# At most two indirect transfers under way, and a plan that reckons with it

## The chip, the cores and the metric

The kernel runs on one core of one Trainium2 chip, as one launch. The metric is the device time in microseconds, from three runs of the kernel. A core has TensorE (PE in the profile), VectorE (DVE), ScalarE (ACT) and GpSimd (POOL), each with its own queue of instructions that it executes in order, SyncE (SP), which here only issues transfers, and 16 DMA engines that all queues share.

## What is computed

A tensor of 32 images with 128 channels and 56 x 56 points goes through two layers. Cut to what matters:

```python
x = x + conv3x3(sign(group_norm(x)), sign(w)) * Alpha
t = to_tokens(x)                                  # 3136 tokens of 128 per image
n = layer_norm(t)
kv = sum over tokens of (n @ Wk + bk) * (n @ Wv + bv)
t = t + (n @ Wq + bq) * kv
n = layer_norm(t)
p = softmax(n @ router_w + router_b)              # 8 experts
top 2 of p, made to sum to 1
t = t + sum over the two: p_e * (n @ expert_w[e] + expert_b[e])
out = from_tokens(t)
```

## The kernel before

An image's 3136 tokens stand in 25 chunks of 128 (the last one has 64). Experts are computed in two ways. **Dense**: for the first 12 chunks of the images 0 to 27, and for all 25 chunks of the last four images, every expert is applied to every token, with the gate (0 for most) multiplied in first: the gates are spread over the partitions by a transfer (`bc`, line 1000), VectorE multiplies (`gated`, line 1009), TensorE multiplies with the expert's weights (`ff`, line 1027). **Sorted**: the other 13 chunks of the images 0 to 27 are sorted by their pair of experts. Each row is written to a place of its own in a table in HBM by an indirect transfer, one for each chunk (`scatter`, line 1202: `rows<-tok,row_no`); the images form four groups of 8, 8, 8 and 4; once a group is complete its tiles of 128 rows are loaded, transposed, multiplied with the two experts of their pair (lines 1440 to 1509) and written to a second table `res`; and a second indirect transfer for each chunk (`gather`, line 1272: `back<-res,res_no`) brings each token's row back, which is transposed (`back_ps`, line 1286), copied (`o`, line 1294) and stored.

So there are 28 x 13 = 364 scatters and as many gathers. All are issued by POOL[...]. POOL's other work is the inverse root of the variance of the two layer norms, a power with the exponent -1/2: `rstd1` and `rstd2` of each image, 64 instructions `r<-var,m_half` of line 449. `rstd1` is needed by `scaled` (ACT, line 624) and by `project_out` (ACT, line 762), `rstd2` by the routing (`route_1`, DVE, line 836) and what follows from it: gates, places of rows, scatters.

The order of work is made in two stages. The kernel records **steps** with `at(due, key, engine, work, ...)`: `work` is the time that the plan reckons on the engine, `delay` what passes after it until others may use the result, `after` what must be done before, and `take`/`free` the buffers it takes and gives back. `in_order` (line 108) goes through the steps as the engines would and brings them into one list: of the steps that can start within 0.3 us of the earliest, the one with the smallest due time comes first. The program is then recorded in that order, and the framework places the instructions on each engine's queue. It takes the recorded order as a preference and not as a rule, so that the built program's order on an engine is not quite that of the plan. The framework also puts in the semaphore waits. The transfers of POOL's queue use eight semaphores in turn, and in the built program a transfer waits for the one eight before it.

Buffers that bear on the change: a gather takes one of six `back` buffers, given back by `back_turn` on PE; the scatters read the token tile `tok`, of which there are three.

Of the kernel before, what the change touches and what calls it, by code (L numbers as in the profile page):

```python
# [67 lines left out]
N_PAIR = N_EXP * (N_EXP - 1) // 2  # L68
N_DENSE = 12
GROUPS = (8, 8, 8, 4)  # L70
TILE_PACE = (0.7, 0.6, 0.4, 0.3)
GATHER_PACE = (1.0, 0.8, 0.5, 0.4)
N_Q = C + 2 * N_EXP
# [82 lines left out]
def conv_attn_moe_kernel(  # L156
# [19 lines left out]
    nc = tc.nc  # L176
# [203 lines left out]
    before = const.tile([C, C], BF16, name="before")  # L380
# [47 lines left out]
    def at(due, key, engine, work, do, *args, after=(), take=(), free=(), delay=0.0):  # L428
        steps[key] = Step(due, key, engine, work, do, args, after, take, free, delay)
# [24 lines left out]
    def plan_image(i: int):  # L454
        s = base(i)
        d = {}
# [41 lines left out]
        def gn_sign(r0, r1):  # L498
# [9 lines left out]
            after=[("load", i - 1)] + ([("gn_sign", 0, GN_PARTS - 1)] if i == 1 else []),  # L508
            take=["x"], delay=9.0 if i else 19.0,
        )  # L510
        for j in range(GN_PARTS):
            rows = j * height // GN_PARTS, (j + 1) * height // GN_PARTS
# [3 lines left out]
                after=[("gn_neg", i), ("conv", i - 1, min(j + 1, n_conv - 1))],  # L516
# [3 lines left out]
            after=[("gn_sum", i, j) for j in range(GN_PARTS)],  # L520
# [4 lines left out]
            after=[("gn_mean", i), ("gn_sign", i - 2, GN_PARTS - 1)], free=[("tr", ("gn_mean", i))],  # L525
# [56 lines left out]
        for b in range(n_conv):  # L582
            at(
                s + 5.5 * b, ("conv", i, b), "PE", 1.75, conv, b,
                after=[("gn_sign", i, j) for j in range(min(b + 2, GN_PARTS))]
# [5 lines left out]
                after=[("conv", i, b)], free=[("mm", ("conv", i, b))],  # L591
            )
        for g in range(n_blk):
            b = min(n_conv - 1, (cols_of(g)[1] - 1) // (ROWS * width))
            due = s + 4 + 5.5 * b
# [3 lines left out]
                after=[("conv_add", i, b), ("xt", i, g - 1)],  # L599
# [4 lines left out]
                after=[("xt", i, g)], free=[("tr", ("xt", i, g))],  # L604
# [3 lines left out]
                after=[("xt_out", i, g), ("var1", i - 2)],  # L608
# [3 lines left out]
            after=[("stats1", i, g) for g in range(n_blk)]  # L612
            + [("project_out", i - 2, 8), ("rstd1", i - 2)],
        )
        at(s + 44, ("rstd1", i), "POOL", 4.5, rstd1, after=[("var1", i)])


        def scaled(g):
# [83 lines left out]
        for g in range(n_blk):  # L702
# [3 lines left out]
                after=[("rstd1", i), ("scaled", i, g - 1), ("scaled", i - 1, last_b)], take=["y"],  # L706
# [3 lines left out]
                after=[("scaled", i, g), ("gram", i, g - 1), ("kv_7", i - 1)],  # L710
# [4 lines left out]
            after=[("gram", i, last_b), ("kv_8", i - 1)], free=[("acc", ("gram", i, 0))],  # L715
# [5 lines left out]
        for j, (engine, work, do) in enumerate(kv_steps, 1):  # L721
            after = [(f"kv_{j - 1}", i) if j > 1 else ("gram_out", i)]
# [9 lines left out]
        for g in range(n_blk):  # L732
# [3 lines left out]
                after=[("kv_4", i), ("scaled", i, g), ("stats1", i, g)],  # L736
# [46 lines left out]
        for j, cs in enumerate(q_groups):  # L783
# [4 lines left out]
                after=[("kv_8", i), ("project", i, j - 1)] + biased, take=["mm"],  # L788
# [4 lines left out]
                after=[("project", i, j)], take=["qs"], free=[("mm", ("project", i, j))],  # L793
# [131 lines left out]
        def gate_parts():  # L925
# [22 lines left out]
            after=[("project_add", i, j) for j in range(last_q + 1)]  # L948
            + [("dense_gates", i - 2), ("row_scalars", i - 2)],
        )  # L950
        at(s + 119, ("rstd2", i), "POOL", 4.5, rstd2, after=[("var2", i)])
        at(s + 125, ("route_1", i), "DVE", 0.85, route_1, after=[("rstd2", i)] + routed)
        at(s + 126, ("route_2", i), "DVE", 1.7, route_2, after=[("route_1", i)])
        at(s + 128, ("route_3", i), "DVE", 1.53, route_3, after=[("route_2", i)])
# [4 lines left out]
            after=[("route_5", i), ("gate_turn", i - 1)],  # L959
# [3 lines left out]
            after=[("dense_gates", i)], take=["tr"],  # L963
# [3 lines left out]
            after=[("gate_turn", i), ("gate_parts", i - 1), ("spread", i - 2, n_units - 1)],  # L967
            delay=3.0,
# [3 lines left out]
            after=[("gate_out", i)], free=[("tr", ("gate_turn", i))], delay=4.0,  # L972
# [72 lines left out]
        for b in dense_blocks:  # L1045
            share = (cols_of(b)[1] - cols_of(b)[0]) / WIDE
            n = b * pairs
            at(
                begin + n * unit - 4, ("tt_turn", i, b), "PE", 0.45 * share, to_channels, b,
                after=[("project_add", i, c // Q_GROUP) for c in blocks[b]]  # L1050
# [6 lines left out]
                after=[("tt_turn", i, b)], free=[("tr", ("tt_turn", i, b))],  # L1057
            )
            for k in range(pairs):
                n = b * pairs + k  # L1060
                at(
                    begin + n * unit - 12, ("spread", i, n), "SP", 0.1 + 0.3 * (k == 0), spread, b, k,
                    after=[("gate_out", i), ("spread", i, n - 1), ("spread", i - 1, last_unit)]
# [5 lines left out]
                    after=[("spread", i, n), ("tt_out", i, b)]  # L1069
# [6 lines left out]
                    after=[("gated", i, n), ("experts", i, n - 1)],  # L1076
# [5 lines left out]
                after=[("experts", i, n)],  # L1082
# [7 lines left out]
        group = group_of[i]  # L1090
# [106 lines left out]

        def scatter(c):
            n = rows_of(c)
            alone(  # L1200
                f"rows{group}",
                nc.gpsimd.indirect_dma_start(  # L1202
                    out=groups[group]["rows"],
                    out_offset=bass.IndirectOffsetOnAxis(
                        ap=d["row_no"][:n, c - N_DENSE : c - N_DENSE + 1], axis=0
                    ),
                    in_=d["tok"][:n, c, :],
                    in_offset=None,
                ),
            )  # L1210

        at(
            s + 132, ("pair_of", i), "DVE", 0.87, pair_of,
            after=[("route_3", i), ("row_numbers", i - 1), ("places", i - 1), ("result_rows", i - 14)],
# [3 lines left out]
            after=[("pair_of", i), ("count_rest", i - 1), ("list_1", group - 1)], take=["to"],  # L1218
# [5 lines left out]
            after=[("places", i), ("count_on", i), ("scatter", i - 2, n_ck - 1)],  # L1224
# [4 lines left out]
            after=[("route_5", i), ("row_add", i - 2, n_ck - 1)],  # L1229
        )  # L1230
        for k, c in enumerate(range(N_DENSE, n_ck)):
            at(
                s + 138 + 3 * k, ("row_add", i, c), "ACT", 0.30, row_add, c,
                after=[("row_scalars", i), ("row_numbers", i), ("project_add", i, c // Q_GROUP)],
                take=["sent"],
            )
            at(
                s + 140 + 3 * k, ("scatter", i, c), "POOL", 1.6, scatter, c,
                after=[("row_add", i, c), ("row_numbers", i), ("open", group)],
                free=[("tok", ("xt", i, 0)), ("sent", ("row_add", i, c))], delay=3.0,  # L1240
            )
        if first_of_group:
            at(
                s + 100, ("open", group), "SP", 0.2, open_group, group,
                after=[("prepare_sorted",), ("rstd1", i)]
# [23 lines left out]
        def gather(c):  # L1269
            d["back", c] = bpool.tile([C, C], F32, tag="back", bufs=6, name=f"back_{i}_{c}")  # L1270
            n = rows_of(c)
            nc.gpsimd.indirect_dma_start(  # L1272
                out=d["back", c][:n, :],
                out_offset=None,
                in_=groups[group]["res"][: quads_of(group) * WIDE, :],
                in_offset=bass.IndirectOffsetOnAxis(
                    ap=d["res_no"][:n, c - N_DENSE : c - N_DENSE + 1], axis=0
                ),
            )

        def back_turn(b):
            lo, hi = cols_of(b)
# [8 lines left out]
        def back_out(b):  # L1291
# [5 lines left out]
        begin, each = gather_due(group)  # L1297
        due = begin + each * (i - last_of[group] + GROUPS[group] - 1)
        at(
            due - 8, ("result_rows", i), "DVE", 1.55, result_rows,  # L1300
            after=[("list_2", group), ("gather", i - 2, n_ck - 1), ("result_rows", i - 1)],
        )
        k = 0
        for b in range(N_DENSE // PER, n_blk):
            share = len(blocks[b]) / PER
            for c in blocks[b]:
                at(
                    due + each * k / n_sort, ("gather", i, c), "POOL", 1.6, gather, c,
                    after=[("result_rows", i)]
                    + [("gather", i, c - 1) if k else ("gather", i - 1, n_ck - 1)]  # L1310
                    + [("tile_out", group, q) for q in range(quads_of(group))],
                    take=["back"], delay=3.0,
                )
                k += 1
            at(
                due + each * k / n_sort + 5, ("back_turn", i, b), "PE", 0.45 * share, back_turn, b,
                after=[("gather", i, c) for c in blocks[b]], take=["tr"],
                free=[("back", ("gather", i, c)) for c in blocks[b]],
            )
            at(  # L1320
                due + each * k / n_sort + 6, ("back_out", i, b), "ACT", 0.47 * share, back_out, b,
                after=[("back_turn", i, b)], free=[("tr", ("back_turn", i, b))],
            )


    groups = {}

    def alone(key, dma):

        tc.declare_no_dep(dma.ins, group=key, reason="writes rows of its own")  # L1330
        tc.add_to_no_dep_group(key, dma.ins)

    def tiles_of(g):
        return (GROUPS[g] * img_rows + N_PAIR * (C - 1)) // C

# [296 lines left out]
```

## Time and profile before

| | |
|---|---|
| time, median of 3 runs (lowest to highest) | 2934.11 us (2931.47 to 2934.41) |
| profiled execution: span, mean granted TensorE clock | 2897.8 us, 0.904 |
| PE busy | 2345.1 us, 81% |
| DVE busy | 1982.0 us, 68% |
| ACT busy | 1348.4 us, 47% |
| POOL busy | 1105.6 us, 38% |
| DMA, mean over the span | 161 GB/s |

A row of the profile's table of groups gives a line, an engine and an operation, how often it ran, its busy time and mean duration, and the idle time of the engine just before it with what ended that idle time. For a transfer that POOL issues the duration is that of the issuing instruction; when the data has landed is not part of it. The list of waits gives, for an engine and a line, what it waited for, the sum in us, how often, and the longest.

### The profile page before, as it was taken

The numbers are of one execution on the slowest core, as the hardware profiler recorded it, in microseconds if no ns is written. First come the engines' busy times: TensorE is split into PE (matmuls) and PEld (weight loads), VectorE is DVE, ScalarE is ACT, GpSimd is POOL, SyncE is SP. The second block draws the span as 40 slices with busy tenths as digits, with TensorE's granted clock in tenths as the row PEclk, the third lists the DMA queues.
The fourth block names the chain that finished last, engine by engine and source line by source line (L and its number), as shares of the span: only waits on it lengthen the run. The fifth ranks groups of instructions, "written<-read, shape, count | busy, mean of one in ns | idle before, by whom it ended". The sixth has DMA issues, their size and how long they took to land. (4 is left out here: it accounts for less than half of the span.)

```text
span 2897.8 us, 43587 instructions
## 1 busy us (share of the span) xinstructions
PE 2345.1 (81%) x11990; PEld 1537.8 (53%) x11990; DVE 1982.0 (68%) x5998; ACT 1348.4 (47%) x4211; POOL 1105.6 (38%) x908
## 2 busy tenths in 40 slices
PE   5888987788788788768887878878778768989777
PEld 3555554455555565536555655545556544655433
DVE  3887877687767678656667657667657657777564
ACT  5564544455544455434555455544446344443210
POOL 1352433321222224443433343665533244233454
PEclk9999999998898899889898989989989988989889
DMA  3354444455444454444554454545645455756476
GB/s 133 107 169 137 159 150 141 140 171 161 143 142 148 139 169 150 149 156 148 161 159 152 146 153 157 169 158 174 184 130 185 138 165 181 227 162 223 160 232 219
DMA packets 309729, 467.06 MB, mean 161 GB/s; under 512 B 61129, under 2 KB 209009, under 8 KB 309490
## 3 DMA queue, kind: packets, MB, share of 16 engines
q1 hardware_dynamic: 285186, 414.11, 45.0%
q0 software_dynamic: 23296, 46.64, 5.4%
q10 hardware_dynamic: 1008, 3.54, 0.4%
q8 instruction: 100, 1.64, 0.2%
q14 instruction: 139, 1.14, 0.1%
HBM read 345.73 MB, written 118.39 MB: 160 GB/s over the span
## 5 line engine op out<-in xcount | busy, mean ns | idle before, releaser
L1027 PE MATMUL ff<-gated,ew_d 128*128 128x512 f32 (+1 forms) x1792 | 895.5, 634 | 123.7 <-DVE gated L1009 123.0
L1272 POOL DMA_INDIRECT back<-res,res_no x364 | 412.6, 1133 | 688.4 <-PE back_ps L1286 551.0
L1202 POOL DMA_INDIRECT rows<-tok,row_no x364 | 395.9, 1088 | 561.5 <-ACT gt_parts L918 174.6
L1027 PEld LDWEIGHTS ff<-gated,ew_d 128*128 128x128 f32 x1792 | 345.4, 207 | 479.2 <-issue 296.2
L1009 DVE TENSOR_TENSOR gated<-tt,bc 128x1024 f32<-128x1024 f32 (+1 forms) x448 | 526.4, 1182 | 92.5 <-PE ff L1027 45.4
L449 POOL TENSOR_TENSOR r<-var,m_half 128x25 f32<-128x25 f32 x64 | 287.6, 4499 | 534.1 <-DVE var L445 516.0
L533 PE MATMUL cv<-xs,w_bin 128*128 128x448 bf16 x2016 | 454.1, 373 | 25.3 <-ACT xs L499 11.2
L624 ACT ACTIVATE y<-tok,r 128x128 f32<-128x128 f32 (+1 forms) x800 | 251.8, 394 | 202.3 <-POOL r L449 180.1
L762 ACT ACTIVATE qs<-q,r 128x136 f32<-128x136 f32 (+1 forms) x800 | 244.7, 388 | 197.2 <-PE q L748 170.3
L533 PEld LDWEIGHTS <-w_bin 128*128 128x128 bf16 x2016 | 206.1, 103 | 211.7 <-issue 73.2
L1465 PE MATMUL to<-ew_s,turned 128*128 x1856 | 263.7, 289 | 49.2 <-ACT turned L1453 32.2
L1465 PEld LDWEIGHTS to<-ew_s,turned 128*128 128x128 f32 x1856 | 243.7, 201 | 94.3 <-ACT turned L1453 43.1
L1480 ACT ACTIVATE v<-to,t_in 128x128 f32<-128x128 f32 x464 | 184.8, 456 | 230.0 <-PE to L1465 124.2
L748 PE MATMUL q<-move,x 128*128 128x144 f32 (+1 forms) x1600 | 251.5, 296 | 15.7 <-ACT move L691 5.1
L748 PEld LDWEIGHTS q<-move,x 128*128 128x128 f32 (+1 forms) x1600 | 222.0, 193 | 62.8 <-issue 32.1
L633 PE MATMUL gram<-y 128*128 128x129 f32 (+1 forms) x1600 | 219.9, 284 | 22.0 <-ACT y L624 22.0
L1492 DVE SCALAR_TENSOR_TENSOR v<-to,t_in,v 128x128 f32<-128x128 f32 x464 | 139.2, 342 | 141.3 <-ACT v L1480 102.9
L633 PEld LDWEIGHTS gram<-y 128*128 128x128 f32 (+1 forms) x1600 | 202.9, 195 | 60.7 <-ACT y L624 30.7
L544 DVE SCALAR_TENSOR_TENSOR x<-cv,alpha_col,x 128x448 f32<-128x448 f32 x224 | 150.8, 675 | 103.1 <-remote 43.9
L573 DVE BATCH_NORM_STATS2 st<-tok 128x6 f32<-128x128 f32 (+1 forms) x800 | 177.8, 276 | 52.1 <-ACT tok L566 30.2
L566 ACT COPY tok<-xt 128x512 f32<-128x512 f32 (+1 forms) x224 | 121.2, 558 | 156.9 <-PE xt L560 78.9
L781 DVE BATCH_NORM_STATS2 st<-tok 128x6 f32<-128x128 f32 (+1 forms) x800 | 180.3, 275 | 0.0
(208 smaller groups left out, 2787.8 us busy)
## 6 DMA issues: line engine op xcount, KB each, us to landing
bc<-gp SPq DMA_DIRECT2D x432, 512.0 KB
x<-in_x_dram SPq DMA_DIRECT2D x64, 784.0 KB
t_in<-rows SPq DMA_DIRECT2D x464, 66.0 KB
res<-v SPq DMA_DIRECT2D x116, 256.0 KB
out_dram<-tt SPq DMA_DIRECT2D x108, 256.0 KB
out_dram<-o SPq DMA_DIRECT2D x84, 256.0 KB
gt<-gb SPq DMA_DIRECT2D x324, 24.0 KB
rows<-zeros SPq DMA_DIRECT2D x116, 66.0 KB
```

What stands on the lines that cost most here:

```text
L449: nc.gpsimd.tensor_tensor(dst, var, m_half.to_broadcast([C, n_ck]), ALU.pow)
L533: nc.tensor.matmul(cv, lhsT=w_bin[:, t, :], rhs=xs[:, b * ROWS + dy : b * ROWS + dy + ROWS, dx : dx + width], start=(t == 0), stop=(t == T ...
L624: nc.scalar.mul(y[:n, j, :C], d["tok"][:n, c, :C], d["r1"][:n, c : c + 1])
L633: nc.tensor.matmul(d["gram"], lhsT=y[:n, j, :C], rhs=y[:n, j, :], start=(c == 0), stop=(c == n_ck - 1),)
L748: nc.tensor.matmul(p[:n, k, :], lhsT=d["x"][:, c * C : c * C + n], rhs=move, start=True, stop=True,)
L762: nc.scalar.mul(qs[:n, k, : C + N_EXP], p[:n, k, : C + N_EXP], d["r1"][:n, c : c + 1])
L1009: nc.vector.tensor_tensor(g[:, :, :n], d["tt", b][:, :n].unsqueeze(1).to_broadcast([C, 2, n]), d.pop(("bc", b, k))[:, :, :n], ALU.mult,)
L1027: nc.tensor.matmul(d["ff", b][:, :n], lhsT=ew_d[:, e * C : (e + 1) * C], rhs=g[:, j, :n], start=False, stop=(e == N_EXP - 1),)
L1202: nc.gpsimd.indirect_dma_start(out=groups[group]["rows"], out_offset=bass.IndirectOffsetOnAxis(ap=d["row_no"][:n, c - N_DENSE : c - N_DENS ...
L1272: nc.gpsimd.indirect_dma_start(out=d["back", c][:n, :], out_offset=None, in_=groups[group]["res"][: quads_of(group) * WIDE, :], in_offset= ...
L1465: nc.tensor.matmul(p[:, k, j, :], lhsT=t[:, n * C : (n + 1) * C], rhs=ew_s[:, bass.ds(d["cols", q][j][n], C)], start=True, stop=True,)
L1480: nc.scalar.activation(d["v", q][:, 2 * h + k, :], d["to", q, h][:, k, 0, :], AF.Identity, bias=row[:, C + 2 : C + 3], scale=row[:, C : C ...
```

## The change

The change has three parts.

1. `in_turn` adds to every indirect transfer a dependence on the one two before it (`IN_FLIGHT = 2`): it is issued only when that one has landed, so that at most two are under way. It holds for scatters and gathers together, in the order in which they are recorded.
2. The plan reckons 2.0 us of POOL's time for a scatter or a gather, where it was 1.6.
3. The plan lets 3.0 us (`rstd1`) and 6.0 us (`rstd2`) pass after the power before its result counts as ready; it was 0.

The second and third part change no instruction. They change the order in which steps are recorded. What it is for: that the transfers do not stand in each other's way, and that the plan places the work after the powers where the chip will have their results.

```diff
+IN_FLIGHT = 2
...
-        at(s + 44, ("rstd1", i), "POOL", 4.5, rstd1, after=[("var1", i)])
+        at(s + 44, ("rstd1", i), "POOL", 4.5, rstd1, after=[("var1", i)], delay=3.0)
...
-        at(s + 119, ("rstd2", i), "POOL", 4.5, rstd2, after=[("var2", i)])
+        at(s + 119, ("rstd2", i), "POOL", 4.5, rstd2, after=[("var2", i)], delay=6.0)
...
         def scatter(c):
...
+            dma = nc.gpsimd.indirect_dma_start(
...
+            alone(f"rows{group}", dma, in_turn(dma))
...
-                s + 140 + 3 * k, ("scatter", i, c), "POOL", 1.6, scatter, c,
+                s + 140 + 3 * k, ("scatter", i, c), "POOL", 2.0, scatter, c,
...
         def gather(c):
...
+            dma = nc.gpsimd.indirect_dma_start(
...
+            in_turn(dma)
...
-                    due + each * k / n_sort, ("gather", i, c), "POOL", 1.6, gather, c,
+                    due + each * k / n_sort, ("gather", i, c), "POOL", 2.0, gather, c,
...
+    def in_turn(dma):
+
+        before = moved[-IN_FLIGHT:][:1] if len(moved) >= IN_FLIGHT else []
+        for b in before:
+            tc.add_manual_dep(dma.ins, b.name, in_turn_dep, reason="few under way")
+        moved.append(dma.ins)
+        return before
```

More of the change, by code (lines that the diff above doesn't have):

```diff
@@ L1199, in scatter @@
             n = rows_of(c)
[L1200 to L1208, printed above, removed]
-                ),
+            dma = nc.gpsimd.indirect_dma_start(
+                out=groups[group]["rows"],
+                out_offset=bass.IndirectOffsetOnAxis(
+                    ap=d["row_no"][:n, c - N_DENSE : c - N_DENSE + 1], axis=0
+                ),
+                in_=d["tok"][:n, c, :],
+                in_offset=None,
             )
+            alone(f"rows{group}", dma, in_turn(dma))
         at(
@@ L1271, in gather @@
             n = rows_of(c)
-            nc.gpsimd.indirect_dma_start(
+            dma = nc.gpsimd.indirect_dma_start(
                 out=d["back", c][:n, :],
@@ L1326, in conv_attn_moe_kernel, with alone @@
     groups = {}
-    def alone(key, dma):
-        tc.declare_no_dep(dma.ins, group=key, reason="writes rows of its own")
+    def alone(key, dma, keep=()):
+        tc.declare_no_dep(dma.ins, group=key, keep=list(keep), reason="writes rows of its own")
         tc.add_to_no_dep_group(key, dma.ins)
+    in_turn_dep = mybir.DependencyInfo(mybir.DependencyClass.Sync, mybir.DependencyReason.DATA)
+    moved = []
+    def in_turn(dma):
[4 more added lines that the diff above has]
+        return before
     def tiles_of(g):
```

## The prediction

> **What bounds the kernel now.** I read the page's busy times first, then the groups of POOL's queue, then the list of waits. From the page (busy us, share of the span, instructions), and then its three groups of POOL:
>
> ```profile
> PE 2345.1 (81%) x11990; PEld 1537.8 (53%) x11990; DVE 1982.0 (68%) x5998; ACT 1348.4 (47%) x4211; POOL 1105.6 (38%) x908
> ...
> L1272 POOL DMA_INDIRECT back<-res,res_no x364 | 412.6, 1133 | 688.4 <-PE back_ps L1286 551.0
> L1202 POOL DMA_INDIRECT rows<-tok,row_no x364 | 395.9, 1088 | 561.5 <-ACT gt_parts L918 174.6
> L449 POOL TENSOR_TENSOR r<-var,m_half 128x25 f32<-128x25 f32 x64 | 287.6, 4499 | 534.1 <-DVE var L445 516.0
> ```
>
> PE is the busiest engine and idles 2898 - 2345 = 553 us; POOL works 38% of the span. POOL is not the bound: a change to its queue counts only through those who wait for POOL. They are in the list of waits (us in total, times, longest):
>
> ```profile
> ACT y L624 <- POOL r L449: 180.1, 32, 15.3
> DVE logit L836 <- POOL r L449: 165.8, 30, 10.6
> PE ff L1027 <- DVE gated L1009: 123.0, 37, 11.5
> PE back_ps L1286 <- DMA back<-res,res_no: 43.9, 20, 6.2
> PE gram L633 <- ACT y L624: 22.0, 14, 4.5
> ```
>
> ACT waits for `rstd1` 32 times, 5.6 us each, and DVE for `rstd2` 30 times, 5.5 us each: little more than one power of 4.5 us. So the powers seldom stand behind transfers; their own duration is waited for, once an image. PE feels this second hand: 123 us for `gated` (DVE stands in the routing), 22 us behind `scaled`. The gathers are waited for by PE only 44 us; mostly POOL waits for PE to give `back` buffers back (551 us).
>
> How long is a transfer under way? The trace's records of the software queue (23296 packets, 32 for each of the 728 transfers) show 16 of data and 16 of 4 bytes that close a transfer. From the start of POOL's instruction to the last closing packet a scatter takes 2.0 us (median; 90%: 3.4), a gather 3.2 us (90%: 5.7). At the start of an instruction 0, 1, 2, 3, 4, 5 earlier ones are still under way 97, 428, 147, 35, 20 and 1 times. So 203 of 728 would meet the new limit; the other 525 would not.
>
> **What the Trainium skill says.** "DMA: Bandwidth & Descriptors", section on the anatomy of one DMA on the SWDGE path, puts the fixed cost at about 2.0 us, mostly completion, and says that DMA engines do not wait on semaphores: a wait is made by the issuing sequencer. The 2.0 us of a scatter agrees; the gathers' 3.2 us is more. That a wait holds POOL itself no transfer here shows, as the wait for the one eight before never binds (five at most are under way); I take it as stated: what stands behind a held transfer on POOL is held too. "Perfetto Trace Analysis", section on SWDGE DMA instructions, says that the instruction ends with its descriptors and not with the data; the trace agrees (a gather's median is 0.96 us against 3.2). So the queue can run at 1.26 us a transfer (0.96 and a gap of 0.30 in the timeline), faster than two under way allow for gathers: 3.2 / 2 = 1.6.
>
> **The change part by part.**
>
> *The limit.* It adds no work. The semaphore wait itself sits on a sequencer that has gaps of 0.3 us, and I cost it at 0 to 0.1 us, hidden in the 62% of the span in which POOL is idle. The cost is the holding. I walked down POOL's timeline, kept each duration, each landing time and each start that something else had released, and moved a transfer back until the one two before had landed (0.1 us for the signal). 170 transfers wait, 40 us in all at scatters and 139 us at gathers. Idle time after a burst takes most of it up. What stays: a scatter starts 0.8 us later on average, a gather 2.5, a power 1.5.
>
> Who sits behind: **scatters** have room. The tile `tok` that a scatter reads is written again 31 to 122 us after the image's last scatter, so their delay costs nothing. **Powers**: 15 of 61 start over 2 us later, 90 us in all, between 1121 and 1293 us and 1767 and 1939 us, where the queue is fullest. Half of it meets ACT (`rstd1`), half DVE (`rstd2`). Of ACT's wait 22/180 = 12% shows on PE: 5 us. Of DVE's I take 30% (123 us of PE's waiting for `gated` against DVE's 166 us for powers, 141 for `v` in line 1492 and 93 ahead of `gated`): 14 us. **Gathers**: elsewhere they run ahead by six buffers; in the last 200 us there is no other image's work to hide behind, and 80 gathers stand there. In the walk the last one starts 6 us later, at most 12 in between: 6 us. Sum 5 + 14 + 6 = 25 us with landing times unchanged.
>
> Two things make it less. A gather issued with three or more under way lands after 4.1 us, with one under way after 3.0: part of what the limit takes it gives back, as the transfers delayed each other. And the built program doesn't have the same crowding: in place of 13 scatters and then 8 gathers it often has scatters and gathers mixed (two of one, two of the other), and scatters land faster. I halve the 25 us: 12. Ends: 0 (landings as before) and 25.
>
> *2.0 us for a transfer in the plan.* No instruction more; it brings the mixing. Mixed, a scatter can stand behind a gather that waits for a `back` buffer; with the room above this is free, but for the last scatter of a group, which releases the tiles. In the built order the tiles of the third group come about one image later, and are made up for in the next (512 against 552 of the tile matmuls at the end of the 27th convolution, 636 against 632 at the 28th). Taken as 0 to 10 us, value 2.
>
> *Slack for the powers.* It should put other work between `var2` and the routing on DVE. The plan does: 9.2 us an image in place of 5.8. But the framework's placing doesn't keep it: in the built program the routing stands directly behind `var2` in 16 of 32 images before and 16 after, with 19 us of work in between in all before and 25 after. That is 6 us less waiting on DVE, some 2 on PE. On ACT the work between the last token copy and the first `scaled` is 6.0 us an image before and 5.1 after: 32 x 0.85 x 12% = 3 us more. Together +1.
>
> *Order in the large.* Counted at the ends of the convolutions, the built orders have the same expert, tile and return matmuls done to within a few, but for the images 25 to 27 and 31. The gaps in the order without a `gated` or an expert matmul are alike. So I expect no large shift from it: 0, with 15 us to either side.
>
> Sum: 12 + 2 + 1 + 0 = +15 us, and 4 off for PE: its mean clock is 0.904, with 0.87 in the busy stretch from 1200 to 1500[...]. 2934 + 11 = 2945 us.
>
> **The rivals.** *Slightly slower (40%)*: the sum above, 2945. *Faster (38%)*: the reordering is worth more than the walk shows. For: the powers are waited for 180 + 166 us, and orders move on every engine, though not as the plan means. If a third of these waits went, 0.30 x 55 + 0.12 x 60 = 24 us would go: 2910. Against: the built order puts no more between power and user than before. *Hidden (12%)*: POOL's idle 62% takes it all and the order balances: 2934. *Clearly slower (10%)*: around the images 25 to 27 the new order has two stretches on PE of 52 and 63 us without an expert matmul, where the longest after the start was 34; (52 + 63) - 2 x 34 = 47 us of expert work that has to be made up: 2985. Against: the stretches hold other PE work.
>
> **How the numbers follow.** Predicted is the likeliest, 2945. The range reaches from beyond the faster case (2900) to the clearly slower one (2985). Faster by over 0.2% (below 2928): the second case, 0.38. Slower (above 2940): the first and last, 0.50. Same 0.12.
>
> **What would show it.** POOL's groups with more idle time before the indirect transfers, ended by a landing; transfers under way at most two, gathers landing in about 3.0 us and the long ones rarer; DVE's wait for the power still some 5.5 us thirty times; PE's wait for `back` up from 44 us by 10 to 30, mostly after 2700 us. It is wrong if the waits for the powers fall by a third or more (then the slack reached the queues), if PE's idle time falls, or if PE's wait for `back` stays at 44 us while the time rises (then it is the order).

## The result

The change made the kernel slower: 3022.91 us (median of 4 runs, 3017.04 to 3029.98) against 2934.26 us for the kernel before (2931.47 to 2945.1, a fourth run included), a ratio of 1.0296 with a 95% interval of 1.0258 to 1.0334. Predicted were 2945 us in a range of 2900 to 2985: the side was right, the size was not, and the time lies outside the range.

The rows of the profile of after that answer to those shown of before, first from the page (busy us, share of the span and instructions; for the groups busy us and mean ns, then the idle time ahead of them and what ended most of it):

```profile
PE 2332.3 (77%) x11990; PEld 1535.9 (51%) x11990; DVE 1975.5 (65%) x5998; ACT 1352.9 (45%) x4211; POOL 1151.2 (38%) x908
...
L1201 POOL DMA_INDIRECT rows<-tok,row_no x364 | 445.3, 1223 | 882.4 <-issue 320.8
L1271 POOL DMA_INDIRECT back<-res,res_no x364 | 414.4, 1138 | 786.5 <-PE back_ps L1286 392.4
L450 POOL TENSOR_TENSOR r<-var,m_half 128x25 f32<-128x25 f32 x64 | 281.9, 4410 | 199.1 <-DVE var L446 183.0
```

PE and DVE don't work longer, and POOL's 46 us more (1105.6 to 1151.2) leave it at 38%. PE idles 3026.0 - 2332.3 = 694 us where it was 553. POOL's idle time has moved: ahead of scatters from 561.5 to 882.4 us, ahead of gathers from 688.4 to 786.5, and ahead of the powers *down* from 534.1 to 199.1. A power that no longer finds POOL idle is a power that stands in a queue. The list of waits shows who pays (us in total, times, longest):

```profile
ACT y L625 <- POOL r L450: 374.5, 29, 30.5
...
DVE logit L837 <- POOL r L450: 236.1, 28, 26.4
...
POOL rows L1201 <- DMA rows<-tok,row_no: 190.8, 77, 7.3
PE ff L1028 <- DVE gated L1010: 189.7, 31, 25.3
...
DVE res_no L1266 <- DMA back<-res,res_no: 162.2, 15, 24.1
...
POOL back L1271 <- DMA back<-res,res_no: 116.0, 53, 5.3
...
PE back_ps L1286 <- DMA back<-res,res_no: 95.4, 39, 10.0
```

ACT's wait for the power has doubled (180 to 375 us), DVE's grew from 166 to 236, PE's for `gated` from 123 to 190 and PE's for `back` from 44 to 95. DVE's wait at `res_no`, the tile with the row numbers of the gathers, grew from 46 to 162: it is written again only when earlier gathers that read it have landed. Almost new are POOL's own waits for a landing, 191 us at scatters and 116 us at gathers (3 us each before).

What this looks like in one image, on POOL's timeline of after (start, duration; in brackets the idle time before it and what the profile names as its end):

```profile
410.75 1.23 POOL L1201 DMA_INDIRECT rows<-tok,row_no  x1 [1.65 <-ACT qs L767]
413.31 0.96 POOL L1201 DMA_INDIRECT rows<-tok,row_no  x1 [1.33 <-ACT xs L500]
419.10 0.96 POOL L1201 DMA_INDIRECT rows<-tok,row_no  x1 [4.83 <-ACT junk L480]
420.37 0.96 POOL L1201 DMA_INDIRECT rows<-tok,row_no  x1 [0.30 <-issue]
425.22 0.96 POOL L1201 DMA_INDIRECT rows<-tok,row_no  x1 [3.89 <-DMA rows<-tok,row_no]
426.48 0.90 POOL L1201 DMA_INDIRECT rows<-tok,row_no  x1 [0.30 <-issue]
427.41 8.63 POOL L450 TENSOR_TENSOR r<-var,m_half 128x25 f32<-128x25 f32 x2
```

The same in the profile of before:

```profile
439.78 0.96 POOL L1202 DMA_INDIRECT rows<-tok,row_no  x1 [0.30 <-issue]
441.05 0.90 POOL L1202 DMA_INDIRECT rows<-tok,row_no  x1 [0.30 <-issue]
467.93 9.37 POOL L449 TENSOR_TENSOR r<-var,m_half 128x25 f32<-128x25 f32 x2 [25.98 <-DVE var L445]
```

Before, the scatters follow each other every 1.27 us and are done 26 us ahead of the next powers. After, they take 1.3 to 5.8 us each, and both powers follow directly behind the last one: the room is used up. The names in brackets mislead here: the scatter at 419.10 is put down to ACT's `junk`, but the transfer two before it landed at 418.01 (from the records of the software queue), and it starts 1.09 us after that. Over the run, 348 transfers start less than 1.5 us after the landing of the one two before, and in the median of these POOL starts 1.17 us after it. A power started on average 1.26 us after the end of the `var` it reads before the change, and 6.05 us after it (64 powers, 81 us in all against 387).

**Two levels of the kernel before.** Beside the experiments, the kernel before took 2660 to 2665 us on three chips and 2925 to 2941 us on a fourth, while after took 3020 us on one of the three and 3023 us in the result above; so a ratio is compared only with ratios whose kernel before stood at the same level. The result above is at the higher one. The trace says where the difference sits. The list of waits of before has rows which the prediction didn't read:

```profile
ACT tt L989 <- remote: 93.9, 12, 19.9
...
ACT v L1480 <- remote: 44.4, 6, 11.9
DVE x L544 <- remote: 43.9, 10, 9.3
...
ACT tok L566 <- remote: 42.9, 6, 12.7
```

"remote" is a wait that ended with a signal for which the profile finds no sender. All such rows of before come to 337 us; after has none, and neither has before at the lower level. In all 65 of these waits the signal is the one that PE's instructions give, and it comes 1.6 to 11.0 us (median 4.1) after the end of the last PE instruction that gives one (such ends are modelled by the profile). So, as far as the records show, DVE, ACT and POOL wait for PE's signals, which come late. It happens in bursts of transfers: 51 of the 59 such waits of DVE and ACT have three or more indirect transfers issued within them and the 3 us ahead of them, the other eight one or two. DVE in before, then PE and SyncE's queue over the same stretch:

```profile
646.93 0.61 DVE L1492 SCALAR_TENSOR_TENSOR v<-to,t_in,v 128x128 f32<-128x128 f32 x2 [0.86 <-issue]
653.17 0.23 DVE L678 SCALAR_TENSOR_TENSOR kr<-rw_sb,kvc_ps,ones 128x8 f32<-128x8 f32 x1 [5.63 <-remote]
```
```profile
644.90 0.28 PE L672 MATMUL kvc_ps<-ident,kv 128*128 128x1 f32 x2
...
653.46 0.60 PE L686 MATMUL kr_ps<-kr,wq_t 128*128 128x8 f32 x2 [5.66 <-DVE kr L678]
```
```profile
640.61 1.36 SPq L938 DMA_DIRECT2D gb<-gt_parts  x3
654.03 0.38 SPq L1509 DMA_DIRECT2D res<-v  x1
```

PE had finished the `kvc_ps` that `kr` reads at 645.2 us. Still DVE, ACT and PE all stand from 647.8 to 653, PE because it needs `kr`, and SyncE issues nothing for 12 us. In the same time POOL issues a scatter every 1.26 us, each with just one earlier one under way. At the lower level DVE goes from the same `v` to the same `kr` without a gap. With these stretches the kernel before loses some 10 us an image between the 5th and the 24th image. So two things differ after the change where the result above was taken: POOL's queue is held, and this standing still is gone. The experiments size both.

### The profile page after: what moved, and what is told of

It reads as the page before. It is cut to its first block, busy times and chain, and to the rows that moved or that the text cites. A ratio compares the mean times of both kernels' runs of the same rounds, so it can differ in the third digit from the quotient of the medians.

```text
span 3026.0 us, 43562 instructions
## 1 busy us (share of the span) xinstructions
PE 2332.3 (77%) x11990; PEld 1535.9 (51%) x11990; DVE 1975.5 (65%) x5998; ACT 1352.9 (45%) x4211; POOL 1151.2 (38%) x908
## 5 line engine op out<-in xcount | busy, mean ns | idle before, releaser
L1201 POOL DMA_INDIRECT rows<-tok,row_no x364 | 445.3, 1223 | 882.4 <-issue 320.8
L1271 POOL DMA_INDIRECT back<-res,res_no x364 | 414.4, 1138 | 786.5 <-PE back_ps L1286 392.4
L1028 PEld LDWEIGHTS ff<-gated,ew_d 128*128 128x128 f32 x1792 | 351.5, 210 | 594.5 <-issue 341.1
L534 PE MATMUL cv<-xs,w_bin 128*128 128x448 bf16 x2016 | 437.1, 363 | 35.4 <-ACT xs L500 18.6
L450 POOL TENSOR_TENSOR r<-var,m_half 128x25 f32<-128x25 f32 x64 | 281.9, 4410 | 199.1 <-DVE var L446 183.0
L534 PEld LDWEIGHTS <-w_bin 128*128 128x128 bf16 x2016 | 199.9, 100 | 220.9 <-issue 74.4
L749 PE MATMUL q<-move,x 128*128 128x144 f32 (+1 forms) x1600 | 261.5, 304 | 22.6 <-ACT qs L767 11.1
L749 PEld LDWEIGHTS q<-move,x 128*128 128x128 f32 (+1 forms) x1600 | 230.0, 200 | 70.8 <-issue 34.6
L775 DVE TENSOR_TENSOR tok<-tok,qs 128x384 f32<-128x384 f32 (+1 forms) x288 | 148.6, 516 | 58.4 <-ACT qs L763 33.4
```

The costliest lines, as they stand in the source:

```text
L450: nc.gpsimd.tensor_tensor(dst, var, m_half.to_broadcast([C, n_ck]), ALU.pow)
L534: nc.tensor.matmul(cv, lhsT=w_bin[:, t, :], rhs=xs[:, b * ROWS + dy : b * ROWS + dy + ROWS, dx : dx + width], start=(t == 0), stop=(t == T ...
L749: nc.tensor.matmul(p[:n, k, :], lhsT=d["x"][:, c * C : c * C + n], rhs=move, start=True, stop=True,)
L1028: nc.tensor.matmul(d["ff", b][:, :n], lhsT=ew_d[:, e * C : (e + 1) * C], rhs=g[:, j, :n], start=False, stop=(e == N_EXP - 1),)
L1201: dma = nc.gpsimd.indirect_dma_start(out=groups[group]["rows"], out_offset=bass.IndirectOffsetOnAxis(ap=d["row_no"][:n, c - N_DENSE : c - ...
L1271: dma = nc.gpsimd.indirect_dma_start(out=d["back", c][:n, :], out_offset=None, in_=groups[group]["res"][: quads_of(group) * WIDE, :], in_o ...
```

## The experiments

Below, *order* is the place that an instruction gets in its engine's queue, and *hold* the waiting for a landing. The letters for theories in the quoted expectations are set anew from group to group: `limit_only`, `plan_only`, `order_dep` and `four` share one set. These four speak in us of a kernel before of 2934, and met one of 2660; what is compared is the ratio.

**1. The parts by themselves (kernel before at 2660 us).** The limit with the old plan:

```diff
-                s + 140 + 3 * k, ("scatter", i, c), "POOL", 2.0, scatter, c,
+                s + 140 + 3 * k, ("scatter", i, c), "POOL", 1.6, scatter, c,
```

and likewise the gather's 2.0 back to 1.6, and both `delay`s taken out.

> The limit of two under way, on the plan of before (1.6 us, no slack). Theory A, holding: a held transfer starts 1.1 us after the landing it waits for, so that 13 scatters take some 35 us in place of 17 and the powers stand behind them; then most of the 89 us is here: 2990 to 3020, ACT's wait for the power well above 300 us. Theory B, order: the plan's new numbers make the loss; then 2935 to 2950 here. Theory C, only together: the plan takes 12 of the 26 us between the last scatter and the next power, the hold takes 17; then the first 15 images stay as before here (the gap is 9 us still), and the time is 2950 to 2980.

Measured: 2903.25 us, ratio 1.0913 (1.0878 to 1.0947). The plan without the limit (`IN_FLIGHT = 1000`):

> The plan's numbers of after (2.0 us, slack of 3 and 6 us) without the limit. Theory A: 2925 to 2950, the powers wait 1 to 2 us as before. Theory B: 3000 to 3025. Theory C: 2935 to 2960, with row numbers 12 us later after the routing's start, as in after, but the powers not held.

Measured: 2727.2 us, 1.0257 (1.0226 to 1.0289). Of the plan only the 2.0 us for a transfer:

> Of the change only the 2.0 us in the plan. Theory A: 1.00 to 1.01, since no transfer is held and scatters have room. Theory B: 1.02 to 1.03.

Measured: 2686.29 us, 1.0075 (1.0048 to 1.0102). Of the plan only the slack of the powers:

> Of the change only the slack of 3 and 6 us. Theory A: it moves the row numbers away from the routing and so costs part of the plan's 2.6%: 1.01 to 1.02. Theory B, that the plan's loss is from the 2.0 us for a transfer: 1.00.

Measured: 2692.61 us, 1.0105 (1.0081 to 1.0129). The kernel after beside them:

> The changed kernel once more, beside the others. If the two causes of the four runs above add up (plan 2.6%, limit 9.1%), 1.10 to 1.13 times the kernel before where that takes 2660 us; where that takes 2934 us, 1.03. Theory A, holding: the powers wait about 390 us in all again.

Measured: 3020.48 us, 1.1337 (1.1305 to 1.1369). And the code of after with `IN_FLIGHT = 1000` and the old plan, which is the program of before:

> The kernel before, written with the code of after: the limit set so high that it adds no dependence, 1.6 us and no slack; its instructions stand in the order of before. Expected: the time of the kernel before within 0.3% on the same chip. Its trace is what the four runs above are to be compared with, since the kernel before took 2660 us beside them and 2934 us beside the changed kernel. If that gap is of the chip and not of the program, the busy times of the engines will be as before and the waits shorter.

Measured: 2662.42 us, 0.9988 (0.9977 to 1.0000). So the edited code costs nothing as such. The plan costs 2.6%, with both of its parts on the wrong side; the limit by itself costs 9.1%; together 13.4%. The mechanism of the limit is in the waits of `limit_only`, which has nearly the order of before on DVE and ACT (in POOL's own queue 165 of 792 places differ):

```profile
ACT y L625 <- POOL r L450: 299.0, 32, 30.1
...
DVE logit L837 <- POOL r L450: 238.1, 30, 20.3
...
PE back_ps L1286 <- DMA back<-res,res_no: 106.6, 39, 11.3
```

against, in `before_same_order`,

```profile
ACT y L625 <- POOL r L450: 175.2, 32, 15.2
...
DVE logit L837 <- POOL r L450: 155.6, 30, 9.0
...
PE back_ps L1286 <- DMA back<-res,res_no: 60.3, 30, 7.7
```

**2. Order or hold?** The dependence as one of order alone: transfers and everything else stand nearly as in after (80 of the 792 places in POOL's queue differ), but no transfer waits for the one two before it: 274 start before that one has landed.

```diff
-    in_turn_dep = mybir.DependencyInfo(mybir.DependencyClass.Sync, mybir.DependencyReason.DATA)
+    in_turn_dep = mybir.DependencyInfo(mybir.DependencyClass.NoSync, mybir.DependencyReason.DATA)
```

> After, but the dependence on the transfer two before is one of order alone, without a wait: nearly the same order on all engines as after (scatters and gathers mixed), nothing held. Theory A: 2930 to 2960. Theory B: 3010 to 3030, as after. Theory C: 2935 to 2965.

Measured: 2763.22 us, 1.0397 (1.0359 to 1.0435). And after with `IN_FLIGHT = 4`:

> After, with four under way in place of two. In the kernel before, 176 of 728 transfers start with two or more earlier ones under way and only 21 with four or more, so that hardly a transfer is held. Theory A and C: at most a tenth of the loss, 2935 to 2965. Theory B: 3000 to 3025.

Measured: 2792.97 us, 1.0503 (1.0471 to 1.0535). The order costs 4.0% (2.6 of it the plan's), the hold 1.1337 / 1.0397 = 1.090, and a hold at four, which seldom binds, costs one more per cent over the order (its own order is not quite the same). The hold is the larger cause at this level, as theory A said; that the order is nearly free, as A had it, is not so.

**3. Powers behind held transfers, or transfers that come late?** The 64 powers are taken off POOL's queue, and the plan stays. As a stand-in VectorE computes the reciprocal (the square root is left out, so the numbers that all later work gets are other ones).

```diff
-        nc.gpsimd.tensor_tensor(dst, var, m_half.to_broadcast([C, n_ck]), ALU.pow)
+        nc.vector.reciprocal(dst, var)
```

> The kernel before, with the 61 powers taken off POOL's queue: in their place VectorE computes the reciprocal of the variance (this changes the values: the square root is left out, so only the time counts). The order of the transfers is that of before. ACT waits 175 us and DVE 156 us for the powers in the trace of before. Theory A (head of the line: the powers are the only ones on POOL's queue whose user waits) expects about 0.30 x 156 + 0.2 x 175 = 80 us less, 2585 us, ratio 0.97. Theory B (POOL's powers are covered, what counts is when data arrive) expects 0.99 to 1.00. It is the base for the next two runs.

Measured: 2446.37 us, 0.9205 (0.9176 to 0.9235), with the granted clock at 0.966 where `before_same_order` had 0.932, and PE busy for 71 us less, so that a part of this gain may be the clock's.

> The kernel after with the same stand-in (reciprocal on VectorE for the power, the square root left out); every transfer still waits for the one two before, order of transfers as in after. Theory A (the loss is that powers stand behind held transfers in POOL's queue): nearly all of the 13.4% goes; about 2650 to 2700 us, ratio to before 1.00 to 1.015, to the run before_powers_off 1.02 to 1.04. Theory B (the loss is that the transfers themselves deliver late: rows for the tiles, back for PE): 2900 us or more, ratio 1.09 or more. Theory C (the order on the other engines, which the declared dependence moved): 1.04 of before_powers_off plus the hold, about 2780 us, ratio 1.045.

Measured: 2690.72 us, 1.0133 (1.0088 to 1.0179).

> After's plan and after's order of transfers nearly, but the dependence is one of order alone and nothing is held (it cost 1.040 with the powers on POOL); here with the stand-in (reciprocal on VectorE for the power, the square root left out). Theory A: the order cost time because gathers that wait for a back buffer now stand among scatters and before powers; without powers in the queue 2590 to 2630 us, 1.00 to 1.02 of before_powers_off. Theory C: still 1.04 of before_powers_off, about 2690 us.

Measured: 2507.49 us, 0.9436 (0.9403 to 0.9469). By the absolute ratio to before the first theory seems to hold (1.013 was in its interval), but it had underrated what the powers cost the kernel *before*: 8%, not 3%. Against `before_powers_off` after still costs 2691 / 2446 = 1.10, the cost of late transfers that the second theory had in mind (its own figure, 1.09 of before, was missed); the order 1.025 of that, between the two forecasts, and the hold 2691 / 2507 = 1.073. In us: with the powers on POOL the hold costs 3020 - 2763 = 257, without them 183. So at this level some 74 us of the hold are powers that stand behind it, and 183 us are transfers that deliver late. Where these meet the engines, in `after_powers_off`:

```profile
DVE res_no L1266 <- DMA back<-res,res_no: 186.7, 18, 21.3
...
PE back_ps L1286 <- DMA back<-res,res_no: 142.7, 49, 10.2
```

and in `before_powers_off`:

```profile
PE back_ps L1286 <- DMA back<-res,res_no: 62.9, 35, 5.3
...
DVE res_no L1266 <- DMA back<-res,res_no: 45.3, 14, 7.2
```

**4. Gathers alone.** In after, `in_turn` is left on the gathers only:

```diff
-            alone(f"rows{group}", dma, in_turn(dma))
+            alone(f"rows{group}", dma)
```

> The kernel after, but only gathers wait (for the gather two before); scatters are free. Theory A: before a power come mostly the 13 scatters of the image, and these run freely again, so the loss is near that of the plan alone: 1.03 to 1.06, 2740 to 2820 us, and the wait of the powers from the end of var to their start falls from 390 us to 100 to 200. Theory B, with gathers as what PE waits for: 1.09 or more.

Measured: 2819.78 us, 1.0603 (1.0569 to 1.0637); the powers waited 164 us in all from `var` to their start. The time is at the upper end of theory A's range, the wait inside it. Over the plan's 1.0257 the limit on gathers is 3.4% more; the rest of the 13.4% comes when scatters wait too.

**5. The powers in full, and two more edits, at the higher level.** From here on the kernel before took 2941.39 us (2925.07 beside the two runs that are named "again"), so that these runs speak of the level of the result above. Forecasts in us that reckon with 2660 can't be compared; their ratios can. VectorE computes the power in 8 instructions of 0.18 us:

```diff
-        nc.gpsimd.tensor_tensor(dst, var, m_half.to_broadcast([C, n_ck]), ALU.pow)
+        half = spool.tile([C, n_ck], F32, tag="half", name="half")
+        nc.vector.tensor_scalar(half.bitcast(U32), var.bitcast(U32), 1, None, ALU.logical_shift_right)
+        nc.vector.tensor_scalar(
+            dst.bitcast(U32), half.bitcast(U32), -1.0, float(0x5F3759DF), ALU.mult, ALU.add
+        )
+        for _ in range(2):
+            nc.vector.scalar_tensor_tensor(half, dst, -0.5, dst, ALU.mult, ALU.mult)
+            nc.vector.tensor_mul(half, half, var)
+            nc.vector.scalar_tensor_tensor(dst, half, 1.5, dst, ALU.add, ALU.mult)
```

> The kernel before with the powers computed on VectorE instead of POOL, and computed in full this time: a first guess from the bits of the variance and two Newton steps, 8 small instructions in place of one of 4.5 us. The reciprocal as a stand-in gave 0.92 of before. If that gain came from taking the powers out of POOL's queue, it comes back but for VectorE's added work (64 x 8 x 0.17 us = 87 us on an engine that is busy 74%, about a third of it seen): 2470 to 2520 us, ratio 0.93 to 0.945. If it came from the changed values (another clock, other data), 0.97 to 1.00.

Measured: 2732.72 us, 0.9285 (0.9256 to 0.9314).

> The kernel after with the same powers on VectorE in full; each transfer waits for the one two before. Theory A (only powers behind held transfers cost): 1.02 to 1.04 of before_newton, about 2560 us. Theory B (held transfers deliver late to PE and to VectorE's res_no, powers or not): 1.09 to 1.10 of before_newton as with the stand-in, 2710 to 2760 us, that is 1.02 to 1.035 of before.

Measured: 2717.05 us, 0.9233 (0.9184 to 0.9283).

> The kernel before with the powers in full on VectorE, a second time, to have it beside the other level of the kernel before. Where the kernel before takes 2941 us it gave 2733; its trace there has 343 us of waits whose release no record shows, as that of before has, and kernels under the limit have none. If before is at 2660 here: Theory B expects 2470 to 2520 us (0.93 to 0.945), so that after_newton with 2717 us would be 1.08 to 1.10 of it, and most of the limit's cost would lie in late transfers and not in powers. If Theory A holds, 2620 to 2660 us (0.985 to 1.00), and after_newton would be 1.02 to 1.04 of it. If before is at 2941: 2733 again.

Measured: 2727.38 us, 0.9281 (0.9214 to 0.9349), beside a kernel before of 2925.07 us. So the lower level wasn't met, and `before_newton` was not measured there. As a ratio the gain lies at the edge of the first forecast (0.93 to 0.945), and the values are computed in full here, so it isn't owed to changed values; which of the theories on the limit holds at the lower level these runs don't say.

At this level the intervals of the two overlap: with the powers off POOL's queue the change costs nothing that was measured, 2717 against 2733. With them on POOL it costs 3022.91 - 2934.26 = 89 us. The powers' part of the change's cost is the difference of the two, 88.65 + 15.67 = 104 us. At the lower level the same difference is (3020.48 - 2662.42) - (2690.72 - 2446.37) = 114 us with the stand-in, so the two levels come near each other. And that the rest comes to nothing isn't for want of late transfers. From the waits of `before_newton`:

```profile
ACT tt L998 <- remote: 70.9, 9, 18.1
...
DVE x L553 <- remote: 57.8, 13, 11.4
...
PE back_ps L1294 <- DMA back<-res,res_no: 33.5, 17, 7.2
...
DVE res_no L1274 <- DMA back<-res,res_no: 31.9, 10, 6.6
```

and of `after_newton`:

```profile
DVE res_no L1274 <- DMA back<-res,res_no: 189.3, 19, 22.2
...
PE back_ps L1294 <- DMA back<-res,res_no: 145.9, 47, 12.9
```

The waits for `back` and `res_no` grow by 270 us (by 221 with the stand-in in experiment 3), and the waits without a visible sender, 343 us in `before_newton` (336 the second time), are gone in `after_newton`. In the time the two seem to cancel. How much each is worth in time was not measured here; at the other level the whole change costs 2690.72 - 2446.37 = 244 us without the powers, 183 of it the hold.

Then the stand of DVE at `res_no`, with more buffers in after:

```diff
-            d["res_no"] = spool.tile([C, n_sort], U32, tag="res_no", bufs=2, name=f"res_no_{i}")
+            d["res_no"] = spool.tile([C, n_sort], U32, tag="res_no", bufs=6, name=f"res_no_{i}")
```

> The kernel after with six buffers in place of two for res_no, the row numbers of the gathers. In the trace of after VectorE stands 162 us, 15 times and up to 24 us, at the write of res_no until the gathers of the image two before have landed; everything of VectorE is queued behind it. Theory B, with this wait as a large part: 30% of it shows, 50 us less, 0.985 of after, ratio to before 1.115 or lower. If VectorE only waits there for what it would wait for anyway: 1.13, and the wait moves to another line.

Measured: 3013.94 us, 1.0229 (1.0197 to 1.026) of a before of 2941; against after's 3022.91 of the result above 0.3% less, where 1.5% less was one forecast and no gain the other. The wait of 162 us fell to 23, and others took it over:

```profile
ACT y L625 <- POOL r L450: 400.9, 29, 29.7
...
DVE logit L837 <- POOL r L450: 296.2, 28, 28.5
...
PE back_ps L1286 <- DMA back<-res,res_no: 105.1, 40, 7.9
...
DVE res_no L1266 <- DMA back<-res,res_no: 23.2, 4, 8.1
```

It was a symptom: DVE waited for transfers in one place, and now waits for what stands behind them in another. The powers now start 552 us late in all, where it was 387, and the time is no longer for it. Last, the limit on scatters alone:

```diff
             ),
         )
-        in_turn(dma)
```

(in `gather`)

> The kernel after, but only scatters wait (for the scatter two before); gathers are free. Gathers alone gave 1.060, plan alone 1.026, both limits 1.134. If the two add up: 1.134 / 1.060 x 1.026 = 1.10, 2920 us, with powers that start 5 us or more late on average. If it is only the two together that cost (a queue mixed of both): 1.05 or less.

Measured: 2875.28 us, 0.975 (0.9715 to 0.9786).

> The limit for scatters alone, a second time. Where the kernel before takes 2941 us it gave 2875, with 74 us of waits whose release no record shows. If before is at 2660 here: 2800 us, 1.05, if those 74 us are all that goes; 2920 us, 1.10, if the limits on scatters and on gathers add up to 1.134. If before is at 2941: 2875 again.

Measured: 2861.96 us, 0.9749 (0.9689 to 0.9809), again at the higher level. With the scatters held and the plan of after, the waits without a visible sender fall from 337 to 74 us (73 the second time), and the kernel is 2.5% *faster* than before, with the powers still on POOL. So at this level it is when the gathers wait too that the change becomes a loss (1.030 against 0.975; in POOL's queue 156 of 792 places differ as well). That it is the hold of the scatters which ends the standing still is likely but not shown: every kernel measured at this level with a hold has the plan of after too, and the plan without a hold was measured at the lower level only, where there is no such standing. Whether the limits on scatters and gathers add up at 2660 us was not measured.

## Why the prediction was wrong

The step that failed is the cost of the limit, 25 us halved to 12: the powers' part of it, 19 us before the halving, came out at 104; late transfers, put at 6, cost 183 us at the lower level; and a gain from waits that end was put at nothing because it wasn't seen. Term by term:

**The restart of a held transfer** was put at 0.1 us. The landing is followed by 1.1 to 1.2 us before POOL starts (median 1.17 of 348). The trace of before held a hint: from the end of DVE's `row_no` to the first scatter of an image it takes 0.8 us. The same walk down POOL's timeline with 1.1 us in place of 0.1 gives 421 us of waiting instead of 179, and powers that start 236 us later in all instead of 90; measured are 387 - 81 = 306 us. This is the term that failed first, and the walk with it corrected comes near. That a wait holds POOL's whole queue, which no transfer of before could show, is borne out: a power starts 6.05 us after its input where it was 1.26.

**Scatters "have room"**, 31 to 122 us until `tok` is written again: true, and the wrong question. The room that mattered was the 26 us between the last scatter and the powers behind it in POOL's queue. The 13 scatters of an image, which took 16 us, take 29 in the early images and about 50 from the 14th on (medians), and use it.

**5 us for ACT and 14 us for DVE, later halved**, is a mis-sized term: the powers' part came out at 104 us (experiment 5). The powers were later by three times what the walk gave, and on average a late microsecond of theirs goes with a third of a microsecond at the end (104 / 306), not 12% on ACT's half. This is a quotient of totals and no fixed price: with six buffers for `res_no` they came 165 us later still at no cost. That POOL's powers were underrated as a whole is shown by 8% and 7% that their leaving POOL saves in before (experiments 3 and 5): "the powers seldom stand behind transfers; their own duration is waited for" was read rightly, and taken for small.

**Gathers, 6 us, and late scatters at nothing**, left out who else waits for a landing. With the powers off POOL's queue the hold still cost 183 us at the lower level (experiment 3), with DVE's wait at `res_no` and PE's for `back` grown most. The prediction counted gathers only in the last 200 us and didn't name `res_no`; of the 51 us by which PE's wait for `back` grew, 18 came in the last 200.

**The halving**, since transfers "delayed each other", has little support. With at most two under way a gather landed a little sooner, after 3.40 us on average where it was 3.58 (median 2.82, it was 3.15; 3.0 was forecast), but a scatter later, after 3.22 where it was 2.45. Sorted by the traffic of the hardware queues while they are under way, both kernels give nearly the same medians: 2.0 to 2.1 us at up to 50 GB/s, 5.0 to 5.4 at 250 to 400 GB/s. Long landings came with traffic, and that three or more were under way was its companion. The 2.0 us of fixed cost that the prediction took from the Trainium skill ("DMA: Bandwidth & Descriptors", the anatomy of one DMA) is met only at the quiet end of this.

**The plan and the order in the large**, +3 and 0 with 15 to either side, were too small: 1.0257 for the plan and 1.0397 for plan and declared order are 67 and 103 us at the lower level. The rival with two long stretches on PE without an expert matmul, 47 us, is a part of this order and was not tested by itself. One effect of the order shows in the trace: from `logit` to `row_no` it takes 26 to 27 us after and took 15 before in the 5th to 8th image (in later images the two differ less evenly), which moves these images' scatters some 12 us nearer to the next powers.

**The 4 us taken off for PE's clock** were not borne out: the granted clock fell from 0.904 to 0.879, and PE was busy 13 us less all the same. In before PE is busy for 234 us of the first 300 at 0.95 and for 233 us from 1200 to 1500 at 0.87, which gives no ground for the term.

**A term was missing**: the waits without a visible sender, 337 us in the list of waits of before. Since after has none, the cost of the change at the higher level was a small difference of two large amounts, and its small size no proof that the queue has slack. That the side was right is thus luck in part. With the terms measured at the lower level the prediction would have been 13%, some 3327 us, and wrong by more, to the other side.

Right was the direction of some waits: more idle time ahead of POOL's transfers, much of it ended by landings; at most two under way (221 transfers were issued with none and 507 with one); PE's wait for `back` up, by 51 us where 10 to 30 were forecast. Wrong were two signs: DVE's wait for the power, to stay at 5.5 us thirty times, is 8.4 us 28 times (the falsifying sign, waits that fall, went the other way), and long landings didn't become rarer for scatters (90% were within 3.4 us before, 5.3 after).

What stays open: why PE's signals come late in bursts of scatters on one chip and not on three others. In the stretch shown the hardware queues move nothing from 643 to 654 us while the software queue goes on, and records of landings are missing (64% of those of the lower level are there in before, 82% in after, which doesn't stand still); they don't show a cause. The number under way alone isn't it, since the scatters shown were issued with one other under way, inside the limit. The limit changed their pace, and the plan of after the order; no run varied either by itself at this level.

A version better than both came out on the way: the powers in full on VectorE, 0.9285 of before without the limit and 0.9233 with it, at the higher level. At 2660 us only the stand-in was measured (0.9205).

## What to carry to other kernels

A wait that was put on a transfer held what stood behind it in the queue: before adding one, look for the next instruction on that engine that somebody waits for, and measure the room ahead of *it*, not the room of the held work. Price the way from a landing to the start of the held transfer from a trace: at 1.17 us here, the limit stretched a burst from a spacing of 1.27 us to one of 2.2. And read every row of the list of waits before adding a sum: a wait for whose end no sender is named is a cost that may go away unseen.

## What the runs showed of the hardware

- From the landing of a transfer to the start of a POOL instruction that waits for it: 1.17 us in the median of the 348 that start within 1.5 us; of all transfers of after 1% start sooner than 1.03 us.
- In before and after an indirect transfer landed after 2.0 to 2.1 us (median) with up to 50 GB/s on the hardware queues, and after 5.0 to 5.4 us at 250 to 400 GB/s; the number of indirect transfers under way made no steady difference beside that.
- A 128x25 power took 4.4 to 4.5 us on POOL; the same by a guess from the bits and two Newton steps took 8 x 0.18 = 1.4 us on DVE, and the kernel before became 7% faster.
- On one chip of four the same program of before took 10% longer, with signals of PE that came up to 11 us late and DVE, ACT, PE and SyncE standing in bursts of scatters spaced 1.26 us. With scatters held to two under way and the plan of after, 1.9 us apart in the median, 74 of the 337 us of such waits were left; with both kinds held, 2.2 us apart, none. Whether the hold or the plan did it is not shown.
